# Two masked attention layers on one core: the first batch's load and scaling order, and the last batch's input steps

## The chip, the cores and the metric

The program runs on one core of one Trainium2 chip. The metric is the device time of one execution in microseconds (us); lower is better. The core has five engines that run side by side, each working through its own list of instructions strictly in the order in which the program wrote them: TensorE (PE in the profile; its weight loads are PEld), VectorE (DVE), ScalarE (ACT), GpSimd (POOL) and SyncE (SP), which here only issues DMAs. An instruction that waits for another engine or for a DMA holds up everything behind it on its own engine.

## The reference

Sixteen batches of 1024 rows by 256 features go through two layers. Each layer normalises its input, cuts it at zero, runs masked attention (4 heads of 64 in layer 0, 8 heads of 32 in layer 1) and adds the result to the input:

```python
h = jnp.maximum(_layernorm(x, axis=-1), 0.0)
x = x + gnn0(h, adj)
h = jnp.maximum(_layernorm(x, axis=-1), 0.0)
x = x + gnn1(h, adj)
# gnn: q, k, v = h @ Wq (+bq), h @ Wk (+bk), h @ Wv (+bv), split by heads
scores = jnp.where(adj > 0, q @ k.T / sqrt(D), -inf)
out = softmax(scores) @ v, heads joined, @ Wo.T + bo
```

Everything is 32-bit. `adj` is an integer matrix of 1024 by 1024 for each batch, the same for both layers.

## The kernel before

**Attention steps.** The main work is a list of steps (`layer_steps`): 16 for layer 0 of a batch, 32 for layer 1. A batch's rows are two halves of 512; a step takes one group of heads, one half of the queries, and two key tiles of 128 (layer 0) or one (layer 1, four heads at a time). `scores` (L501) multiplies keys by queries into two PSUM pairs called `ps`; the pool of such pairs has three buffers, shared by all large products. `exponentials` puts the mask on each pair on VectorE (L524, output `p`) and then takes the exponential on ScalarE (L530). `weigh` (L542, output `po`) multiplies the exponentials with the values, two steps later. The sums of the exponentials are made by GpSimd adding tiles in pairs (L659), by an adding DMA that GpSimd issues (`accumulate`, L643), and by a product with ones on TensorE (`count`, L387, output `pz`). They then travel: copied by ScalarE (`spread`, tile `s`), moved by DMA (`sums`), inverted on VectorE (`vn`), sent out and fetched back by DMA (`vd`, `inv`), and multiplied into the output on GpSimd (`normalize`, L447, tile `cat`). `end_half` (L483, `py`) multiplies `cat` with Wo.

**Order of the steps.** Layer 0 of batch 0, then in turn layer 0 of batch b+1 and layer 1 of batch b, and at last layer 1 of batch 15. Below, c is the first step of layer 1 of batch 14, and e = c + 32 the first of layer 1 of batch 15.

**Work laid between the steps.** `later(i, f, ...)` puts a piece of work at step i. `Stream.run` (L588) writes step by step: scores; the weighing of earlier steps; counts; the exponentials; then the pieces due at this step, first those that `rank` does not name and then those that it does (`turn` and the `LARGE` ones: `k`, `q`, `values`, `end_half`). Layer 0 takes two steps at a time, so pieces due at steps 0 and 1 are written together. On an even step of layer 1 that carries a `LARGE` piece the weighing is put off to the next step. There is no scheduler behind this: the order written is the order run.

**Inputs of a layer** (`Inputs`, one for each batch and layer, work by halves): `stats` (L198, L199 on VectorE for each of four row tiles, then four small operations on GpSimd, L209 to L212, that give `rstd` and `shift`); `norm` (ScalarE, L221) or `scale` (VectorE, L243) into `hn`; a transposition to `hT`, either on TensorE (`turn`, `turn_scaled`, output `ph`, copied out by ScalarE and VectorE at L260 and L261) or in blocks on VectorE with two DMA trips (`turn_blocks`, `put_blocks`, `place_blocks`); then `k`, `q` (L304, `pq`) and `values` (L345, `pv`), each copied out of PSUM. `add_bias` (L230, GpSimd) adds the output bias to the rows.

**Masks.** `Mask.load` fetches one eighth of `adj` with four DMAs; `put` (L167, ScalarE) packs it; `flip` (L173, VectorE) transposes blocks; `second` (L178, ScalarE) rewrites it for layer 1. The first step needs eighths 0 to 3.

**The head** (L738 to L789, before the steps): loads are issued on SP, save eighths 1 and 3 of the first mask, which ScalarE issues. `idle(n)` (L755) is n products of the identity with itself into a tile that nothing reads. Then half 0 of batch 0 gets its statistics, `norm` for three tiles and `scale` for the fourth, `turn_scaled`, `k`, `q`; half 1 gets statistics, `scale` and `turn_scaled`, and its `k`, `values` and `q` are laid at steps 0 and 2. `norms(inputs[0][1], 0, 1, ...)` (L851) lays the first statistics of batch 1 at step 1.

**The tail's inputs** (the `else` at L889): statistics, `norm`, bias, transposition, `k`, `q` and `values` of layer 1 of batch 15 are laid over the 32 steps of layer 1 of batch 14.

Of the kernel before, what the change touches and what calls it, by code (L numbers as in the profile page):

```python
# [24 lines left out]
LARGE = ("k", "q", "values", "end_half")  # L25
# [65 lines left out]
def fast_program(ctx, tc, a, w, loads, chk):  # L91
# [3 lines left out]
    nc = tc.nc  # L95
    x, adj, out = a["x"], a["adj"], a["out"]
    B, N, E = x.shape
    NT = N // P
# [35 lines left out]
    def open_x(b, half):  # L134
        t = xp.tile([P, 4, E], F32, tag=f"x{half}", name=f"x_{b}_{half}")
        for g, rows in enumerate(quarters(x, b, half)):
            nc.sync.dma_start(t[ts(g, 32)], rows)
        xs[b, half] = t


    class Mask:
# [3 lines left out]
        def load(self, u, at=None, queue=nc.sync):  # L145

            if at is None:
                at = adjp.tile([P, 4, 256], I32, tag="adj", name=f"adj_{self.b}_{u}")
            self.src[u] = at
            rows = adj[self.b].rearrange("(t h r g) (k c) -> h t k r g c", h=QH, r=32, g=4, k=4)  # L150
            for k in range(4):
                queue.dma_start(at[ts(k, 32)], rows[u // 4, u % 4, k])
# [415 lines left out]
    class Stream:  # L568
# [12 lines left out]
        def later(self, i, f, *args):  # L581
            self.due.setdefault(i, []).append((f, args))

        def rank(self, entry):

            return entry[0].__name__ in ("turn", *LARGE)

        def run(self):  # L588
            steps = self.steps
# [143 lines left out]
    def open_w(n):  # L733
        for _ in range(n):
            t, src = loads.pop(0)
            nc.sync.dma_start(t, src)
# [3 lines left out]
    mask, inp = masks[0], inputs[0][0]  # L740
# [8 lines left out]
    def rewrite(u):  # L749
        mask.put(u)  # L750
        mask.flip(u)
# [3 lines left out]
    def idle(n):  # L755
        for _ in range(n):
            nc.tensor.matmul(warm[:, 0, :P], w.ident, w.ident, start=True, stop=True)

    idle(22)
    open_w(2)  # L760
    for u in (1, 3):
        load(u, nc.scalar)
    open_x(0, 1)
    for u in (0, 2):
        load(u)
    open_w(1)
    for u in range(4, NT):
# [5 lines left out]
    inp.stats(0, (0, 1), True)  # L773
    inp.stats(0, (2, 3), True)
    inp.norm(0, (0, 1, 2), whole=True)
    inp.stats(1, (0, 1))
    inp.scale(0, (3,))
    inp.turn_scaled(0, lambda: idle(7))
    idle(3)
    inp.stats(1, (2, 3))  # L780
    rewrite(0)
    mask.put(1)
    inp.k(0)
    mask.flip(1)
    inp.scale(1, range(4))
    rewrite(2)
    rewrite(3)
    inp.q(0)
    inp.turn_scaled(1)  # L789

    def bias_of_v():

# [22 lines left out]
    later = stream.later  # L815

    def norms(inp, half, *at, whole=False, bias=None):

        for i, f in zip(at, (inp.stats, inp.stats, inp.norm, inp.norm)):
            rest = (whole,) if i in at[2:] else ()  # L820
            later(i, f, half, (0, 1) if i in (at[0], at[2]) else (2, 3), *rest)
        later(at[3] + 1 if bias is None else bias, inp.add_bias, half)

    def half_inputs(inp, half, *at):

        for i, f in zip(at, (inp.turn, inp.k, inp.q, inp.values)):
            later(i, f, half)

    def block_inputs(inp, half, turn, put, place, *at):

        later(turn, inp.turn_blocks, half)
        later(put, inp.put_blocks, half)
        later(place, inp.place_blocks, half)
        for i, f in zip(at, (inp.k, inp.q, inp.values)):
            later(i, f, half)


    for i, f, half in (0, inp.k, 1), (0, inp.values, 0), (0, inp.values, 1), (2, inp.q, 1):
        later(i, f, half)
    for half in range(QH):  # L840
        later(10 + 2 * half, inp.add_bias, half)
# [3 lines left out]
    for t in range(NT):  # L845
        i = 7 + 2 * t
# [8 lines left out]
    for b in range(B - 1):  # L855
        mine, a, c = inputs[1][b], first[b + 1], second[b]
        if b == 0:

            norms(mine, 0, a + 4, a + 6, a + 7, a + 8, whole=True)
            half_inputs(mine, 0, a + 10, a + 12, a + 13, a + 14)  # L860
            norms(mine, 1, a + 10, a + 11, a + 12, a + 13, whole=True)
            half_inputs(mine, 1, a + 15, c, c + 6, c + 2)
        else:
            norms(mine, 0, a - 20, a - 16, a - 15, a - 13, bias=a)
            block_inputs(mine, 0, a - 10, a - 8, a - 4, a, a + 2, a + 8)
            norms(mine, 1, a - 14, a - 10, a - 8, a - 6, bias=a + 6)
            block_inputs(mine, 1, a, a + 6, a + 7, c, c + (6 if b + 2 < B else 10), c + 2)
        for i, u in zip((0, 2, 4, 6, 7, 9, 11, 13), range(NT)):
            later(a + i, masks[b].second, u)
        if b + 2 < B:  # L870
            other, mask = inputs[0][b + 2], masks[b + 2]
            later(a + 6, open_x, b + 2, 0)
            later(c, open_x, b + 2, 1)
            if b == 0:
                norms(other, 0, a + 12, a + 14, c, c + 1, bias=c + 34)
                block_inputs(other, 0, c + 2, c + 3, c + 4, c + 8, c + 16, c + 18)
                norms(other, 1, c + 3, c + 4, c + 6, c + 7, bias=c + 36)
                block_inputs(other, 1, c + 8, c + 9, c + 12, c + 22, c + 26, c + 30)
            else:
                norms(other, 0, a + 10, a + 12, a + 13, a + 15, bias=c + 34)  # L880
                block_inputs(other, 0, c, c + 1, c + 2, c + 8, c + 16, c + 18)
                norms(other, 1, c + 2, c + 4, c + 5, c + 6, bias=c + 36)
                block_inputs(other, 1, c + 7, c + 8, c + 12, c + 22, c + 26, c + 30)
            at = 5, 8, 10, 12, 14, 45, 49, 51, 53
            for t in range(NT):
                later(a + at[t], mask.load, t)
                later(a + at[t + 1], mask.put, t)
                later(a + at[t + 1] + (1 if t == 4 else 2), mask.flip, t)
        else:  # L889
            last, e = inputs[1][b + 1], c + 32  # L890
            norms(last, 0, c + 5, c + 6, c + 8, c + 9)
            block_inputs(last, 0, c + 12, c + 13, c + 14, c + 18, c + 26, c + 20)
            norms(last, 1, c + 18, c + 20, c + 21, c + 22)
            block_inputs(last, 1, c + 24, c + 25, c + 26, e, e + 10, e + 2)
            for i, u in zip((4, 14, 24, 26, 36, 40, 42, 44), range(NT)):
                later(c + i, masks[b + 1].second, u)
    stream.run()

# [155 lines left out]
def kernel(  # L1054
# [28 lines left out]
    with ExitStack() as fast, tc.manual_schedule():  # L1083
        fast_program(fast, tc, a, w, loads, chk)
# [61 lines left out]
```

## Time and profile before

| what | value |
|---|---|
| median of three runs | 3099.81 us (3097.14 to 3100.33) |
| profiled execution, its own time | 3096.61 us |
| its span in the profile | 3094.8 us |
| VectorE, ScalarE, GpSimd busy | 2474.6, 2230.1, 2436.5 us |
| mean granted TensorE clock | 0.999 |
| median time from issue to landing, `adj` and `x` loads on SP | 3.0 and 3.1 us |
| one batch in the steady part (steps of batch 3 to 4, layer 0 to layer 0) | 189.6 us |

The span is the time from the first to the last recorded instruction; some 1.8 us of the execution lie outside it. In the profile's lists a row reads: start, duration (both us), engine, line, operation, output and inputs, shapes, number of instructions merged, and in brackets the engine's idle time before it with what ended it. A "q" behind an engine's name is its sequencer, which issues a DMA. Matmuls of 32-bit data appear as more than one record each. Matmul ends are modelled, so a stretch in which TensorE waits between two products of one group can still count as busy.

### The profile page before, as it was taken

The page shows a single profiled execution, that of the slowest core. Times are in us where ns is not written, and L with a number is a line of the kernel's source. Part 1 is how long each engine was busy: PE and PEld are TensorE (multiplying, and loading weights), DVE is VectorE, ACT ScalarE, POOL GpSimd, SP SyncE. Part 2 cuts the span into 40 slices and gives each one's busy share as a digit, 9 for nine tenths or more (in the row PEclk, how much of TensorE's full clock was granted, in tenths as well). Part 3 has the DMA queues.
Part 4 walks back from the last instruction along what each step waited for, and adds up shares of the span by engine and source line. Part 5 has one row for each costly group of instructions (what it writes and reads, how often), then busy time and mean ns, then how long its engine had stood idle before and what let it go on. Part 6 is the DMA issues. An engine that isn't in the chain of part 4 may idle for free.

```text
span 3094.8 us, 47328 instructions
## 1 busy us (share of the span) xinstructions
PE 3074.0 (99%) x17406; PEld 1221.3 (39%) x17406; DVE 2474.6 (80%) x2698; ACT 2230.1 (72%) x2436; POOL 2436.5 (79%) x1554
## 2 busy tenths in 40 slices
PE   9999999999999999999999999999999999999998
PEld 4443433434334343343434334343343433434333
DVE  6778788887888878788787888878788787887777
ACT  5677777777777777778677677776777777776676
POOL 3578878787887878878788787887878778787787
PEclk9999999999999999999999999999999999999999
DMA  5215545454463544635445353554535545453331
GB/s 129 66 58 118 127 106 129 121 112 119 107 137 110 119 118 103 143 108 117 120 103 134 107 127 110 113 127 110 127 110 111 132 105 125 120 112 84 79 77 33
DMA packets 259230, 341.37 MB, mean 110 GB/s; under 512 B 58288, under 2 KB 218288, under 8 KB 241968
## 3 DMA queue, kind: packets, MB, share of 16 engines
q0 software_dynamic: 19152, 139.47, 22.6%
q1 hardware_dynamic: 238368, 197.51, 22.2%
q8 instruction: 138, 2.26, 0.3%
q10 hardware_dynamic: 1472, 1.31, 0.2%
q14 instruction: 100, 0.82, 0.1%
HBM read 149.95 MB, written 47.96 MB: 64 GB/s over the span
## 4 chain that ended last, share of the span: by engine, by line
PE 95%; DVE 2%; POOL 1%; DMA 1%; issue 1%; ACT 0%; SPq 0%; DVEq 0%; ACTq 0%; POOLq 0%
PE ps L501 31%; PE po L542 29%; PE pq L304 15%; PE pv L345 8%; PE py L483 7%; PE pz L387 4%; DVE p L524 1%; POOL p L659 1%; DMA inv<-vd 0%; DMA x<-in_x_dram 0%; SPq L420 0%; ACT p L530 0%; DMA sums<-s 0%; POOL cat L447 0%; DMA adj<-in_adj_dram 0%
## 5 line engine op out<-in xcount | busy, mean ns | idle before, releaser
L524 DVE SCALAR_TENSOR_TENSOR p<-mask,ps 128x1024 f32<-128x1024 fp8e5 x1536 | 1791.9, 1214 | 366.2 <-PE ps L501 348.5
L530 ACT ACTIVATE p<-p 128x1024 f32<-128x1024 f32 x1536 | 1607.0, 1056 | 628.1 <-DVE p L524 572.1
L659 POOL TENSOR_TENSOR p<-p,p 128x1024 f32<-128x1024 f32 x510 | 1212.8, 2430 | 166.3 <-PE po L542 165.8
L501 PE MATMUL ps<-qT,kT 32*128 32x512 f32 (+1 forms) x6144 | 1073.3, 628 | 3.6 <-DVE p L524 3.0
L542 PE MATMUL po<-p,v 128*32 128x512 f32 (+1 forms) x6144 | 980.2, 600 | 0.7 <-ACT cat L399 0.4
L501 PEld LDWEIGHTS ps<-qT,kT 32*128 32x128 f32 (+1 forms) x6144 | 349.7, 184 | 587.9 <-issue 243.1
L542 PEld LDWEIGHTS po<-p,v 128*32 128x32 f32 (+1 forms) x6144 | 234.3, 118 | 680.3 <-issue 474.5
L555 POOL TENSOR_TENSOR p<-p 128x1024 f32<-128x1024 f32 x128 | 302.7, 2365 | 90.5 <-DVE p L554 85.1
L554 POOL TENSOR_TENSOR p<-p,p 128x1024 f32<-128x1024 f32 x64 | 150.8, 2356 | 169.6 <-DVE p L551 126.3
L345 PE MATMUL pv<-wv,hT 128*128 128x256 f32 x1024 | 237.8, 385 | 0.0
L304 PE MATMUL pq<-hT,wk 128*128 128x512 f32 x512 | 236.7, 605 | 0.7 <-DVE p L524 0.6
L304 PE MATMUL pq<-hT,wq 128*128 128x512 f32 x512 | 236.6, 605 | 0.1
L483 PE MATMUL py<-wo,cat 128*128 128x256 f32 x1008 | 234.4, 386 | 0.7 <-DVE p L524 0.6
L447 POOL TENSOR_TENSOR cat<-cat,inv 128x512 f32<-128x512 f32 x127 | 174.9, 1383 | 73.0 <-DMA inv<-vd 72.6
L345 PEld LDWEIGHTS pv<-wv,hT 128*128 128x128 f32 x1024 | 189.4, 190 | 72.1 <-DVE p L524 21.3
L483 PEld LDWEIGHTS py<-wo,cat 128*128 128x128 f32 x1008 | 186.3, 190 | 74.8 <-issue 25.1
L551 DVE TENSOR_TENSOR p<-p 128x1024 f32<-128x1024 f32 x128 | 181.7, 1419 | 0.0
L387 PE MATMUL pz<-p,ones 128*32 128x256 f32 (+1 forms) x1928 | 180.4, 444 | 0.5 <-DMA p<-p 0.5
L643 POOL DMA_DIRECT2D p<-p x133 | 122.6, 922 | 63.7 <-POOL p L659 30.3
L221 ACT ACTIVATE hn<-x,shift,rstd 128x256 f32<-128x256 f32 x251 | 135.6, 588 | 43.7 <-DMA turned<-hn 32.2
L399 ACT COPY cat<-po 128x512 f32<-128x512 f32 x128 | 73.4, 573 | 118.5 <-PE py L483 96.6
L488 DVE TENSOR_TENSOR x<-py,x 128x1024 f32<-128x1024 f32 x63 | 77.1, 1224 | 101.9 <-PE py L483 101.2
(62 smaller groups left out, 1773.1 us busy)
## 6 DMA issues: line engine op xcount, KB each, us to landing
p<-p POOLq DMA_DIRECT2D x133, 1024.0 KB, 7.8
adj<-in_adj_dram SPq DMA_DIRECT2D x504, 128.0 KB, 3.0
turned<-hn SPq DMA_DIRECT2D x58, 512.0 KB, 3.8
hT<-turned SPq DMA_DIRECT2D x232, 128.0 KB, 2.8
x<-in_x_dram SPq DMA_DIRECT2D x128, 128.0 KB, 3.1
inv<-vd SPq DMA_DIRECT2D x128, 128.0 KB, 3.0
inv<-vd SPq DMA_DIRECT2D x252, 64.0 KB, 3.3
out_dram<-x SPq DMA_DIRECT2D x124, 128.0 KB, 2.3
```

What stands on the lines that cost most here:

```text
L304: nc.tensor.matmul(pq[:, m, :], wt[self.layer][:, c, ts(m, P)], self.hT[half][:, c, :], start=(c == 0), stop=(c == 1),)
L345: nc.tensor.matmul(pv[:, i, :], self.hT[half][:, c, ts(i, P)], w.v[self.layer][:, c, :], start=(c == 0), stop=(c == 1),)
L387: nc.tensor.matmul(self.s[ts(r, 32), q], w.ones.to_broadcast([P, 32]), of[:, q], start=start and not part, stop=stop and part != 0,)
L447: nc.gpsimd.tensor_mul(o, o, inv)
L483: nc.tensor.matmul(py[:, i, :], self.half.cat[:, c, ts(i, P)], w.o[self.layer][:, c, :], start=(c == 0), stop=(c == 1),)
L501: nc.tensor.matmul(st.ps[i // 2][:, i % 2, :], gr.inp.kT[r * D : (r + 1) * D, gr.g, ts(kt, P)], gr.inp.qT[gr.qh][r * D : (r + 1) * D, gr.g ...
L524: nc.vector.scalar_tensor_tensor(out=half, in0=gr.mask.m[gr.qh][:, kt // 4, :, kt % 4].unsqueeze(1).to_broadcast([P, 2, 512]), scalar=-EDG ...
L530: nc.scalar.activation(half, half, AF.Exp, scale=gr.scale)
L542: nc.tensor.matmul(gr.o[r * D : (r + 1) * D, :], gr.inp.v[:, kt, h * D : (h + 1) * D], st.halves[i // 2][:, i % 2, :], start=(kt == 0), st ...
L551: nc.vector.tensor_add(a, a, b)
L555: nc.gpsimd.tensor_add(a, a, b)
L659: nc.gpsimd.tensor_add(half, half, of)
```

## The change

In the head, all loads of the first mask go to SP, eighths 0 and 1 ahead of the second half of `x`, eighths 2 and 3 behind it. The `scale` of the fourth tile comes before any statistics of half 1; those come as one call after the first `k`. The idle products inside the first transposition go from 7 to 3. `turn_scaled` of half 1 leaves the head: two of its tiles are scaled there and two at step 0, and the transposition stands at step 0 behind `values` of half 0 and ahead of `k` of half 1. The mask's `rewrite` calls (a `put` and a `flip` each) stand otherwise among the products. `rank` counts `turn_scaled` with the large pieces.

In the tail, `q` of half 1 of layer 1 of batch 14 goes from step c+10 to c+8. For layer 1 of batch 15 the statistics of a half, laid two tiles at a time at c+5, c+6 and c+18, c+20, become one call at c+8 and at c+20; `norm` goes to c+11, c+12 (half 0) and c+22 (half 1, all four tiles); the bias of half 0 from c+10 to c+13; transposition, DMA out and DMA back from c+12, c+13, c+14 to c+14, c+15, c+16, and from c+24, c+25, c+26 to c+26, c+27, c+28; `k`, `q`, `values` of half 0 from c+18, c+26, c+20 to c+20, c+22, c+26. Two `second` calls are moved.

```diff
         def rank(self, entry):
-            return entry[0].__name__ in ("turn", *LARGE)
+            return entry[0].__name__ in ("turn", "turn_scaled", *LARGE)
...
     idle(22)
     open_w(2)
-    for u in (1, 3):
-        load(u, nc.scalar)
+    for u in (0, 1):
+        load(u)
     open_x(0, 1)
-    for u in (0, 2):
+    for u in (2, 3):
         load(u)
     open_w(1)
     for u in range(4, NT):
...
     inp.norm(0, (0, 1, 2), whole=True)
-    inp.stats(1, (0, 1))
     inp.scale(0, (3,))
-    inp.turn_scaled(0, lambda: idle(7))
+    inp.turn_scaled(0, lambda: idle(3))
     idle(3)
-    inp.stats(1, (2, 3))
     rewrite(0)
-    mask.put(1)
+    rewrite(1)
     inp.k(0)
-    mask.flip(1)
-    inp.scale(1, range(4))
+    inp.stats(1)
     rewrite(2)
+    inp.q(0)
     rewrite(3)
-    inp.q(0)
-    inp.turn_scaled(1)
+    inp.scale(1, (0, 1))
...
-    for i, f, half in (0, inp.k, 1), (0, inp.values, 0), (0, inp.values, 1), (2, inp.q, 1):
+    later(0, inp.scale, 1, (2, 3))
+    for i, f, half in (
+        (0, inp.values, 0), (0, inp.turn_scaled, 1), (0, inp.k, 1), (0, inp.values, 1),
+        (2, inp.q, 1),
+    ):
         later(i, f, half)
...
-            block_inputs(mine, 1, a, a + 6, a + 7, c, c + (6 if b + 2 < B else 10), c + 2)
+            block_inputs(mine, 1, a, a + 6, a + 7, c, c + (6 if b + 2 < B else 8), c + 2)
...
             last, e = inputs[1][b + 1], c + 32
-            norms(last, 0, c + 5, c + 6, c + 8, c + 9)
-            block_inputs(last, 0, c + 12, c + 13, c + 14, c + 18, c + 26, c + 20)
-            norms(last, 1, c + 18, c + 20, c + 21, c + 22)
-            block_inputs(last, 1, c + 24, c + 25, c + 26, e, e + 10, e + 2)
-            for i, u in zip((4, 14, 24, 26, 36, 40, 42, 44), range(NT)):
+            later(c + 8, last.stats, 0)
+            later(c + 11, last.norm, 0, (0, 1))
+            later(c + 12, last.norm, 0, (2, 3))
+            later(c + 13, last.add_bias, 0)
+            block_inputs(last, 0, c + 14, c + 15, c + 16, c + 20, c + 22, c + 26)
+            later(c + 20, last.stats, 1)
+            later(c + 22, last.norm, 1)
+            later(c + 23, last.add_bias, 1)
+            block_inputs(last, 1, c + 26, c + 27, c + 28, e, e + 10, e + 2)
+            for i, u in zip((4, 8, 14, 26, 36, 40, 42, 44), range(NT)):
                 later(c + i, masks[b + 1].second, u)
```

## The prediction

> **What bounds the kernel now.** First the page's busy times and its chain of waits, by engine:
>
> ```profile
> PE 3074.0 (99%) x17406; PEld 1221.3 (39%) x17406; DVE 2474.6 (80%) x2698; ACT 2230.1 (72%) x2436; POOL 2436.5 (79%) x1554
> PE 95%; DVE 2%; POOL 1%; DMA 1%; issue 1%; ACT 0%; SPq 0%; DVEq 0%; ACTq 0%; POOLq 0%
> ```
>
> TensorE is busy 99% and is 95% of the chain: 20.8 us are left to gain in all. The table by stretch says where (columns: stretch, length, busy time and count of PE, PEld, DVE, ACT, POOL, granted clock, DMA share, GB/s):
>
> ```profile
> 0.00:24.20 24.20, 19.92 (x98) 14.85 (x98) 9.34 (x29) 9.10 (x12) 4.81 (x24) 0.93 0.91 218
> 7.96:11.38 3.42, 0.98 (x7) 0.57 (x6) 1.02 (x4) 1.51 (x3) 2.31 (x8) 1.00 1.13 234
> 11.38:14.79 3.41, 3.41 (x17) 3.06 (x15) 1.24 (x5) 0.08 (x1) 0.00 (x0) 0.50 1.12 231
> 2421.80:2611.60 189.80, 189.77 (x1075) 75.03 (x1074) 153.75 (x168) 139.27 (x152) 153.43 (x98) 1.00 0.48 117
> 2875.00:2900.00 25.00, 23.70 (x146) 8.74 (x143) 20.34 (x25) 18.47 (x22) 19.37 (x14) 1.00 0.29 65
> ```
>
> A steady batch has nothing to give: 189.77 of 189.80 us. The head and layer 1 of batch 14 (2858 to 2971) have, and only these are changed. The middle only shifts by what the head gains or loses. Now the head's timeline:
>
> ```profile
> 9.78 5.21 SPq L152 DMA_DIRECT2D adj<-in_adj_dram  x8
> 15.66 10.74 SPq L152 DMA_DIRECT2D adj<-in_adj_dram  x16
> 26.45 2.01 SPq L137 DMA_DIRECT2D x<-in_x_dram  x4
> 13.45 0.43 DVE L198 BATCH_NORM_STATS2 st<-x 128x6 f32<-128x256 f32 x1 [4.36 <-DMA x<-in_x_dram]
> 31.63 0.43 DVE L198 BATCH_NORM_STATS2 st<-x 128x6 f32<-128x256 f32 x1 [1.50 <-DMA x<-in_x_dram]
> 16.25 3.70 PE L304 MATMUL pq<-hT,wk 128*128 128x512 f32 x8
> 24.19 3.74 PE L501 MATMUL ps<-qT,kT 64*128 64x512 f32 x16
> 27.93 3.70 PE L304 MATMUL pq<-hT,wk 128*128 128x512 f32 x8
> 31.46 7.07 PE L345 MATMUL pv<-wv,hT 128*128 128x256 f32 x32
> 38.46 3.70 PE L501 MATMUL ps<-qT,kT 64*128 64x512 f32 x16
> ```
>
> VectorE waits twice for `x`: at 13.45 for half 1 of batch 0, with the fourth tile's `scale` (14.69) behind it, so the first `k` starts only at 16.25; and at 31.63 for batch 1, which costs nothing, since TensorE has `k` and `values` until 38.46.
>
> **The head, part by part.** *Before the first `k`.* The first four `x` loads take 2.5 us to land where they have little company, and the last was late: statistics start at 6.40. Without ScalarE's loads I put that at 4.9 (last issue 2.1 plus 2.6), 1.4 earlier. The later `shift` moves from 10.44 to 9.0, `norm` and `scale` end at 9.6 (0.59 each), 6 idle records take 0.75 (as the 6 at 15.4), the last transposes 0.63, the copy 0.60: first `k` near 11.3, 5 us earlier.
>
> *What eats it.* `k` and `q` (7.1) end at 18.6, scores can start at 19.3. The masks are next: eighth 3 is still the last of the same 3.5 MB and lands near 19.3 (SP issues it until 15.6, plus 3.7); `put` 1.13, `flip` 0.43, two `scale` 0.75 bring the first masking to 21.8, against 25.53. Four maskings (4.6) end at 26.4. `values` of half 0 waits for a pair that the second masking frees (24.1) and ends at 27.8; the transposition, now here, ends at 28.7 (0.87); ScalarE's copy (0.60, behind 1.01 of copying values) at 29.5.
>
> *The new wait.* `k` of half 1 needs both copies of `hT`; VectorE's (L261) is written behind the pieces that `rank` does not name at steps 0 and 1, and one of these is the statistics of batch 1, the row at 31.63. So VectorE stands at a DMA, behind it `hT`, behind that `k` on TensorE, and behind that everything. With a the arrival of that `x`: two statistics 1.33 (31.63 to 32.96), copy 0.73, then three quarters of `k` 2.78 and `values` 3.46, and 0.05 of hand-over: next scores at a + 8.35, against 38.46. The gain of 5 us becomes idle time of TensorE between 30.4 and a + 2.1.
>
> *How late is a?* SP issues the mask at 0.65 each (5.21/8) and takes eight more of them: 5.2. But it stood waiting before: the four `x` loads took 3.81 and another 1.17 passed before 9.78, together with a 0.8 gap ahead of `wq`. Counted anew: `wq` done at 3.5, 5.2 for eight, 2.0 for four `x` (as at 26.45): 10.7 instead of 9.78, and from there the same list. Latency should be a little less on an emptier queue. I take 0.4 later, a = 32.0, head +1.9 (40.35 against 38.46). Bounds: all 5.2 late, a = 36.8, +6.7; or, with the fifty loads of 128 KB up to it (6.55 MB) at the 246 GB/s that the stretch from 1.5 to 8.2 shows with both queues, a = 28.1, where `k` waits for `hT`'s own copies alone (30.4) and the head gains 1.9.
>
> The Trainium skill ("Trainium Kernel Development and Optimization", Key Constraints) holds that issuing DMAs from several engines saves nothing but sequencer time. By it the move would cost at most SP's 5.2, and nothing where the 16 engines are full; the rows show both in part (DMA share 1.13 at 8 to 11 us, 0.64 at 24 to 28), and the counted 0.9, less some latency, stands.
>
> *Clock.* That gap is 3.7 us. In the rows above, 0.98 us of work in 3.42 was followed by 3.41 us at half clock. In the new gap two such lengths hold some 1.1 to 1.2 us of work each (up to 28.7 with 0.9 of `k`; after 34.15). Bounds 0 and 2.3 (both next lengths at half clock while work waits: 0.6 and 1.7). I take 1.7, as the nearest row is the halved one. The skill ("TensorE: Matmul & The Clock Gate", The two states you'll see) wants a whole idle window of about 3.4 us, free-running, before the clock drops; a 3.7 us gap would seldom hold one, and the sum would be 1.7 lower. The row, halved with 29% busy, goes against that reading. Head: +3.6.
>
> **Layer 1 of batch 14.** Its waits, in the timeline:
>
> ```profile
> 2887.40 1.13 PE L501 MATMUL ps<-qT,kT 32*128 32x512 f32 x4 [0.55 <-DVE p L524]
> 2890.88 1.13 PE L501 MATMUL ps<-qT,kT 32*128 32x512 f32 x4 [0.29 <-DVE p L524]
> 2896.51 2.52 POOL L447 TENSOR_TENSOR cat<-cat,inv 128x512 f32<-128x512 f32 x2 [0.41 <-DMA inv<-vd]
> 2903.98 0.91 POOL L643 DMA_DIRECT2D p<-p  x1 [0.30 <-POOL p L659]
> 2906.97 9.60 POOL L659 TENSOR_TENSOR p<-p,p 128x1024 f32<-128x1024 f32 x4
> 2911.99 0.64 PE L387 MATMUL pz<-p,ones 128*32 128x256 f32 x8
> 2913.24 1.13 PE L483 MATMUL py<-wo,cat 128*128 128x256 f32 x4 [0.60 <-DVE p L524]
> ```
>
> Scores stall where VectorE has statistics between maskings; later GpSimd is the pace. Steps 7 and 8 lose about 2.7 us now (ps to po 2.74 and 2.48, against 1.07 unhindered). New: step 6 stays, since `vn` waits for `sums` until 2886.0 with or without statistics ahead; step 7's maskings come 1.2 earlier; step 8 has `q` (3.70) over four statistics (2.7) and the `qT` copy (1.41). Step 11 starts 0.6 earlier than 2901.23. But GpSimd now does `ve` behind all four statistics, which end near 2895.9: 1.6 for L209 to L212, 2.5 for `cat`, 4.7 for the next addition: 2904.75 against 2903.70. The adding DMA is issued 1.05 later and landed 7.3 after its issue; the count that needs it moves from 2911.99 to 2912.45, `py` to 2913.05: 0.2 gained of 1.2. The bias (2.67) behind the next four additions puts the following ones at 2919.4, against 2919.18. In steps 15 to 20, now with no large product, both maskings and additions need 2.35 a step against 2.07 on TensorE; `k` at step 20 covers that. Transposed rows reach `hT` near 2965, `k` wants them after 2970. Sum: -0.5. Bounds: all the idle of 2875 to 2975 gone (3.4: 1.30, 1.32 and 0.82 in its stretches), or both halves with four statistics ahead of GpSimd's queue (1.05 and 1.35 late): +2.4. I stay by the worked row, since GpSimd holds either way.
>
> **Sum.** +3.6 and -0.5: +3.1 on 3096.61, 3099.7; the profiled execution lies 3.2 below the median, so the same shift gives 3102.9.
>
> **The rivals.** *The head's gain survives*: `x` of batch 1 lands by 28.3. For it: 246 GB/s early on; against: 0.65 an issue on one queue, and SP's list before it is the same. -1.9, with the tail -0.5 to -3.4: 3094.5 to 3097.4.
>
> *Slower beyond telling*: SP carries the eight loads in full, a = 36.8. For it: 5.21 us for eight; against: SP's own waits in 3.0 to 9.8. Head +6.7, half clock +1.7, tail -0.5: 3107.7; it decides from a = 35.0 (+4.9 head, with the rest +6.1).
>
> *The tail is not evened*: GpSimd late in both halves, +3.6 +2.4: 3105.8. For it: `ve` ahead of `cat` and the additions; against: GpSimd's idle 2.25 and 1.11 us at 2932 and 2940, which takes the second half's.
>
> **How the numbers follow.** A measurement of this kernel can tell some 0.2%, 6.2 us, from no change. Forecast 0.62 (0.60 within, 0.02 slower), gain survives 0.18 (0.06 faster, where both lower bounds, -5.3 together, meet the 3 us by which runs differ; 0.12 within), late loads 0.13 (0.10 slower, 0.03 within), uneven tail 0.07 (0.02 slower, 0.05 within). Faster 0.06, within 0.80, slower 0.14. Range: low 3095.5, inside the first rival, high 3107, short of the late loads.
>
> **What would show it.** First `k` near 11 to 12; a wait of VectorE for `x` of 4 us or more ahead of L198 near 32, then L261, then `k` of half 1 ending near 37; scores of step 2 near 40.4, perhaps at clock 0.5; step 14's `py` at most 1.2 us earlier relative to the layer's start. If those statistics start by 28, or TensorE has no gap ahead of that `k`, the forecast's mechanism is wrong.

## The result, and the profile after

The changed kernel takes **3105.36 us** (median of 20 runs, 3100.99 to 3107.00); the kernel before, on the same chip, 3097.72 us (20 runs, 3095.62 to 3100.33). The ratio is **1.0022**, with a 95% interval of 1.0015 to 1.0029: slower by 7.6 us, where 3.1 had been forecast. The time lies inside the predicted range (3095.5 to 3107). The loss is over the 6.2 us that the prediction called the least that can be told from no change, but its interval, 4.6 to 9.0 us, holds that bound. The profiled execution took 3104.45 us, its span is 3102.6 us, against 3096.61 and 3094.8 before.

The busy times by engine and the chain of waits by engine, of the kernel after:

```profile
PE 3075.2 (99%) x17398; PEld 1220.8 (39%) x17398; DVE 2467.5 (80%) x2698; ACT 2231.3 (72%) x2436; POOL 2437.9 (79%) x1554
PE 91%; DVE 2%; DMA 2%; POOL 1%; ACT 1%; issue 1%; SPq 1%; DVEq 0%; ACTq 0%; POOLq 0%
```

TensorE is still busy 99% of the span, but its share of the chain went from 95% to 91%: DMAs, ScalarE and SP's queue have each about a point more of it. To see where the time went, the span is cut at four places that both kernels have: the first scores of step 2, of layer 0 of batch 1, of layer 1 of batch 14, and of layer 1 of batch 15. The table by stretch, first of the kernel before, then after (stretch, length, busy time and count of PE, PEld, DVE, ACT, POOL, granted clock, DMA share, GB/s):

```profile
111.99:2858.01 2746.02, 2743.80 (x15385) 1085.59 (x15384) 2229.47 (x2423) 2003.99 (x2192) 2199.14 (x1391) 1.00 0.47 115
2858.01:2970.70 112.69, 109.88 (x707) 39.93 (x705) 87.69 (x92) 80.61 (x88) 95.24 (x57) 1.00 0.38 89
2970.70:3094.80 124.10, 113.01 (x870) 43.15 (x866) 87.24 (x83) 79.94 (x84) 93.53 (x58) 0.98 0.16 39
```

```profile
117.62:2866.44 2748.82, 2744.41 (x15385) 1085.59 (x15384) 2221.71 (x2423) 2004.75 (x2192) 2200.24 (x1391) 1.00 0.47 115
2866.44:2976.59 110.15, 107.82 (x706) 39.32 (x704) 88.02 (x92) 80.90 (x88) 95.18 (x57) 1.00 0.40 90
2976.59:3102.60 126.01, 114.06 (x870) 43.55 (x866) 87.25 (x83) 79.94 (x84) 93.55 (x58) 0.96 0.16 40
```

With the head (scores of step 2 at 38.46 before, 43.94 after) and the short piece up to batch 1 (73.53 and 73.68 us), the 7.8 us between the spans divide as follows:

| part | predicted | seen in the two profiles |
|---|---|---|
| head, up to the scores of step 2 | +3.6 | +5.5 |
| from there to layer 0 of batch 1 | 0 | +0.15 |
| middle, whose code is the same in both | 0 | +2.8 |
| layer 1 of batch 14 | -0.5 | -2.5 |
| layer 1 of batch 15 to the end | 0 | +1.9 |

The head's timeline of the kernel after:

```profile
11.32 3.70 PE L304 MATMUL pq<-hT,wk 128*128 128x512 f32 x8
27.46 2.01 SPq L137 DMA_DIRECT2D x<-in_x_dram  x4
27.29 1.04 PE L259 MATMUL ph<-ident,hn 128*128 128x128 f32 x8
29.05 1.12 PE L304 MATMUL pq<-hT,wk 128*128 128x512 f32 x2 [0.73 <-ACT hT L260]
32.86 0.43 DVE L198 BATCH_NORM_STATS2 st<-x 128x6 f32<-128x256 f32 x1 [6.28 <-DMA x<-in_x_dram]
34.10 0.66 DVE L261 TENSOR_SCALAR hT<-ph 128x512 f32<-128x512 f32 x1
34.81 5.49 PE L304 MATMUL pq<-hT,wk 128*128 128x512 f32 x6 [4.64 <-DVE hT L261]
40.09 3.92 PE L345 MATMUL pv<-wv,hT 128*128 128x256 f32 x16
43.94 3.27 PE L501 MATMUL ps<-qT,kT 64*128 64x512 f32 x14
```

The first `k` starts at 11.32, five microseconds earlier than before. `k` of half 1 starts at 29.05, and after a quarter of it TensorE stands for 4.64 us. The bracket names VectorE's copy of `hT` (L261), which itself took 0.66 us; it stood behind the statistics of batch 1 (L198), and these stood 6.28 us for `x`, which SP issued only at 27.46. The rest of `k` then took 5.49 us for six records, where eight take 3.70: it ran at half clock.

### The profile page after: what moved, and what is told of

Its sections match the earlier page's. It is cut to its first block, busy times and chain, and to the rows that moved or that the text cites. A ratio compares the mean times of both kernels' runs of the same rounds, so it can differ in the third digit from the quotient of the medians.

```text
span 3102.6 us, 47318 instructions
## 1 busy us (share of the span) xinstructions
PE 3075.2 (99%) x17398; PEld 1220.8 (39%) x17398; DVE 2467.5 (80%) x2698; ACT 2231.3 (72%) x2436; POOL 2437.9 (79%) x1554
## 3 DMA queue, kind: packets, MB, share of 16 engines
q8 instruction: 139, 2.28, 0.3%
## 4 chain that ended last, share of the span: by engine, by line
PE 91%; DVE 2%; DMA 2%; POOL 1%; ACT 1%; issue 1%; SPq 1%; DVEq 0%; ACTq 0%; POOLq 0%
PE ps L501 30%; PE po L542 28%; PE pq L304 14%; PE py L483 7%; PE pv L345 7%; PE pz L387 4%; DVE p L524 1%; DMA inv<-vd 1%; DMA sums<-s 1%; POOL p L659 1%; DMA turned<-hn 0%; ACT p L530 0%; SPq L420 0%; DMA p<-p 0%; SPq L439 0%
```

## The experiments

All times are medians beside runs of the kernel before on the same chip. The idle products that some add or take away write a tile that nothing reads.

**1. Statistics of batch 1 one step later.** In the kernel after:

```diff
-    norms(inputs[0][1], 0, 1, 3, 5, 6, whole=True)
+    norms(inputs[0][1], 0, 2, 3, 5, 6, whole=True)
```

> The changed kernel with one number altered: the first statistics of batch 1 laid at step 2 in place of step 1, so that VectorE copies hT of half 1 before it waits for x of batch 1. Wait theory (the loss is VectorE standing at that DMA, then half clock): k of half 1 has no wait over 1 us, no half clock between 30 and 45 us, the scores of step 2 start near 36.3 us against 43.9 in the changed kernel and 38.5 before, and the time falls by about 7.6 us to 3097 to 3099. Load theory (all loads on one queue are late and that is the loss): scores of step 2 still past 42 us and the time stays at 3104 to 3106. Tail theory (the late statistics of batch 15 are the loss): the head improves as above but the time stays over 3102.

Measured: 3096.37 us (11 runs) against 3098.41, ratio 0.9995 (0.9986 to 1.0004). Its head:

```profile
29.39 0.69 DVE L261 TENSOR_SCALAR hT<-ph 128x512 f32<-128x512 f32 x1 [2.45 <-ACT hT L260]
29.41 3.70 PE L304 MATMUL pq<-hT,wk 128*128 128x512 f32 x8 [0.73 <-ACT hT L260]
32.95 3.62 PE L345 MATMUL pv<-wv,hT 128*128 128x256 f32 x16
36.49 3.70 PE L501 MATMUL ps<-qT,kT 64*128 64x512 f32 x16
```

VectorE now copies `hT` at 29.39, as soon as the transposed tiles are there, `k` runs through, and step 2's scores start at 36.49 instead of 43.94. One piece of work laid one step later took away the whole loss: the time is the same as before within its interval. So the wait for `x` of batch 1 costs the head 7.45 us, clock included, and without it the head's new order gains 2 us on the profile of before (38.46).

**2 and 3. Each half of the change alone.** Experiment 2 has the head of before and the tail of after (with `q` at c+8); experiment 3 the head of after and the tail of before.

```diff
 # 3: the tail as before
-            later(c + 8, last.stats, 0)
...
+            norms(last, 0, c + 5, c + 6, c + 8, c + 9)
+            block_inputs(last, 0, c + 12, c + 13, c + 14, c + 18, c + 26, c + 20)
```

> The kernel before with the change's tail alone (head as before). By the traces layer 1 of batch 14 takes 2.5 us less (110.2 against 112.7), so wait theory: 3094 to 3096, 2 to 3 us under before. Tail theory: over before, 3099 or more. If the 1.9 us lost after layer 1 of batch 14 in the changed kernel's trace belongs to the tail, the sum is -0.6 and the time the same as before within a microsecond.

> The kernel before with the change's head alone (tail as before). Wait theory: scores of step 2 near 43.9 us and the time 3103 to 3106 by the head's 5.5 us alone, up to 3108 if the tail's gain of 2.5 us is missing from it. Tail theory: time near before, under 3100.

Measured: tail alone 3095.65 against 3098.41, 0.9991 (0.9982 to 1.0000); head alone 3106.07 against 3098.41, 1.0025 (1.0016 to 1.0034). The tail gains about 2.8 us, though its interval just reaches no change, and the head loses about 7.7, so the loss comes with the head. The two add up to 4.9 us, not to the 7.6 of the whole change. The intervals, some 3 us either way, leave room for that, but the profiles show a part that comes only with both: from layer 1 of batch 15 to the end takes 123.78 us with the tail alone, 124.48 with the head alone and 126.01 and 125.64 in the two profiles of the kernel after. Layer 1 of batch 14 takes 110.90 us with the tail alone and 113.06 with the head alone.

**4. Work in the gap.** In the kernel after, 20 idle products stand between the transposition of half 1 and `k`, in the time in which TensorE waits:

```diff
-        (0, inp.values, 0), (0, inp.turn_scaled, 1), (0, inp.k, 1), (0, inp.values, 1),
-        (2, inp.q, 1),
+        (0, inp.values, 0), (0, inp.turn_scaled, 1), (0, fill, 20), (0, inp.k, 1),
+        (0, inp.values, 1), (2, inp.q, 1),
```

> The changed kernel with 20 idle products (5.5 us) on TensorE between the transposition of half 1 and its k: the wait for hT stays, but TensorE has work in it. If the half clock of 6.8 us after the gap is due to the gap, it does not come, and scores of step 2 start near 41.2 us (32.9 + 8.35) in place of 43.9: 2.5 to 3 us less than the changed kernel, 3102 to 3103. If the clock falls for another reason, no gain: 3105.

Measured: 3099.25 against 3098.41, 1.0000 (0.9991 to 1.0009). This was expected at 3102 to 3103. First the kernel after, by stretches at which the clock can change (in all fourteen profiles a granted clock holds for a multiple of 3.413 us, save the last, which the end cuts off; columns as above):

```profile
27.04:30.45 3.41, 2.41 (x12) 1.24 (x11) 0.00 (x0) 1.51 (x2) 0.00 (x0) 1.00 0.73 229
30.45:33.86 3.41, 0.00 (x0) 0.00 (x0) 0.93 (x3) 0.00 (x0) 0.00 (x0) 1.00 0.70 197
33.86:37.27 3.41, 2.46 (x3) 1.17 (x4) 0.86 (x3) 0.00 (x0) 0.00 (x0) 0.50 0.95 213
37.27:40.69 3.42, 3.42 (x6) 1.52 (x5) 0.00 (x0) 0.35 (x1) 0.00 (x0) 0.50 1.04 309
```

Then the timeline of the experiment, and its stretch from `k` to the scores:

```profile
28.52 4.63 PE L762 MATMUL fill<-ident 128*128 128x128 f32 x40
32.71 0.43 DVE L198 BATCH_NORM_STATS2 st<-x 128x6 f32<-128x256 f32 x1 [5.76 <-DMA x<-in_x_dram]
34.66 2.84 PE L304 MATMUL pq<-hT,wk 128*128 128x512 f32 x6 [0.65 <-DVE hT L261]
37.34 3.62 PE L345 MATMUL pv<-wv,hT 128*128 128x256 f32 x16
```

```profile
34.66:40.89 6.23, 6.23 (x23) 4.10 (x23) 0.00 (x0) 1.01 (x1) 0.00 (x0) 1.00 1.07 287
```

VectorE's statistics start at 32.71, as in the kernel after (32.86), so the wait is the same; but the six records of `k` take 2.84 us instead of 5.49, and the scores start at 40.89. That is 32.71 + 8.18, against the prediction's a + 8.35 with full clock. The empty stretch of 30.45 to 33.86 thus cost the kernel after two lengths of 3.41 us at half clock, and 43.94 - (32.86 + 8.35) = 2.7 us (2.9 by the 8.18). The time fell by more than that: the 20 products also move what stands behind them, and experiments 9 to 12 come back to this.

**5 and 6. The loads alone.** Experiment 5 is the kernel before with only the head's loads in the new order; experiment 6 the kernel after with the loads in the old one.

```diff
 # 5 (6 is the reverse, in the kernel after)
-    for u in (1, 3):
-        load(u, nc.scalar)
+    for u in (0, 1):
+        load(u)
     open_x(0, 1)
-    for u in (0, 2):
+    for u in (2, 3):
         load(u)
```

> The kernel before with only the order of the loads changed: all on SP, eighths 0 and 1 ahead of the second half of x. Wait theory: the loads alone cost nothing that is seen, since x of batch 1 has slack there: its statistics start near 32.9 us in place of 31.6, TensorE does not wait for them, scores of step 2 at 38 to 40 us, time within 1.5 us of before. Load theory (one queue is itself the loss): scores of step 2 past 42 us and the time 4 us or more over before.

> The changed kernel with the loads as they were, on two queues. Wait theory: the wait for x of batch 1 stays, since VectorE's order is the change's, but x comes some 1.2 us sooner: scores of step 2 at 40 us without the half clock, 42.7 to 43.4 with it; time 3102 to 3105, at most 2.5 us under the changed kernel. Load theory: the loss is gone, 3098 or less.

Measured: experiment 5 3100.20 against 3098.21, 1.0005 (0.9996 to 1.0015); experiment 6 3100.05 against 3098.21, 1.0006 (0.9996 to 1.0015). The second was expected at 3102 to 3105: a miss. The first was expected within 1.5 us of before and lies 2.0 over it, with no change inside its interval; its scores of step 2, expected at 38 to 40, start at 41.05, behind two lengths at half clock in its head (13.94 to 20.77) where the kernel before has one. The timelines of 5 and of 6:

```profile
32.70 0.43 DVE L198 BATCH_NORM_STATS2 st<-x 128x6 f32<-128x256 f32 x1
34.05 7.07 PE L345 MATMUL pv<-wv,hT 128*128 128x256 f32 x32
41.05 3.70 PE L501 MATMUL ps<-qT,kT 64*128 64x512 f32 x16
```

```profile
31.45 0.43 DVE L198 BATCH_NORM_STATS2 st<-x 128x6 f32<-128x256 f32 x1 [1.68 <-DMA x<-in_x_dram]
32.24 4.01 PE L304 MATMUL pq<-hT,wk 128*128 128x512 f32 x8 [0.73 <-ACT hT L260]
36.08 3.62 PE L345 MATMUL pv<-wv,hT 128*128 128x256 f32 x16
39.63 2.85 PE L501 MATMUL ps<-qT,kT 64*128 64x512 f32 x12
```

In 5 the statistics start as late as in the kernel after, and TensorE does not stop: nothing that it needs stands behind them. The new loads by themselves cost nothing that could be told from no change. In 6 the wait is there, but the first `k` comes 2.4 us later than in the kernel after (13.73 against 11.32) and `x` 1.4 us earlier (31.45), so the gap closes to fragments, no stretch of 3.41 us has under 2.3 us of work there, and the clock stays. The scores start at 39.63, again a + 8.18. Both kernels also show what the early `k` is made of: with the new loads alone it starts at 17.11, with the new order of work alone at 13.73, with both at 11.32.

**7 and 8. The kernel before and the kernel after once more.**

> The kernel before once more, for a second trace of its middle (from layer 0 of batch 1 to layer 1 of batch 14, code that the change does not touch), which took 2746.0 us in the first trace and 2748.8 in the changed kernel's. If the 2.8 us are run to run spread, this one lies anywhere from 2744 to 2749; if the middle follows the head, 2744.5 to 2746.5.

> The changed kernel once more, for a second trace of its middle, 2748.8 us in the first. If that is spread, anywhere from 2744 to 2749; if the middle follows the head, 2747.5 to 2749.5.

Measured, one execution each: 3099.77 and 3105.0 us. The middle took 2746.20 and 2747.66 us, against 2746.03 and 2748.82 in the first profiles. Two of a kind do not settle it, but every profile with the kernel after's head so far (experiments 1, 3 and 6) had a middle of 2747.87 to 2748.09, every one with the kernel before's (2 and 5) 2744.65 to 2745.29, and experiment 4, with 20 products added to the head of after, 2746.14.

**9 and 10. The number of idle products.** The kernels differ there in one more thing: 7 idle products against 3 inside the first transposition. Experiment 9 is experiment 1 with `idle(7)`, experiment 10 the kernel before with `idle(3)`:

```diff
 # 9, in experiment 1 (10 is the reverse, in the kernel before)
-    inp.turn_scaled(0, lambda: idle(3))
+    inp.turn_scaled(0, lambda: idle(7))
```

> The changed kernel with the first statistics of batch 1 at step 2, as tried before, and with 7 idle products inside the first transposition in place of 3, as in the kernel before. In nine traces the middle (layer 0 of batch 1 to layer 1 of batch 14) took 2744.7 to 2746.2 us where TensorE's program has 7 idle products in its head and 2747.7 to 2748.8 where it has 3, and 2746.1 with 3 and 20 more. Position theory: the middle follows the number of TensorE instructions ahead of it, so 2744.5 to 2746.5 here, and the time falls to 3093 to 3095, under the kernel before by 3 to 5 us. Timetable theory: the middle follows how far ahead or behind the other engines stand after the head, so 2747.5 to 2749 and a time of 3096 to 3097. Scores of step 2 at 36 to 37 us in both.

> The kernel before with 3 idle products in place of 7 inside the first transposition, nothing else. Position theory: its middle takes 2747.5 to 2749 us in place of 2744.7 to 2746.2 and the time rises by 2 to 3 us to 3100 to 3101.5. Timetable theory: middle and time as before (2744.5 to 2746.5; 3097 to 3099).

Measured: experiment 9 **3094.30** (11 runs) against 3098.28, 0.9988 (0.9979 to 0.9997), faster than both kernels; middle 2745.61. Experiment 10 3102.54 against 3098.28, 1.0014 (1.0004 to 1.0023); middle 2747.55. The middles are as the theory of position had them. Experiment 10 lost 4.3 us, more than the 3 expected and more than its middle explains; in its profile layer 1 of batch 14 also has two lengths at half clock and takes 114.94 us, against 112.69 and 113.60 in the profiles of before.

**11 and 12. The same number elsewhere.** To part position from what the products do to the transposition, the warm-up ahead of everything gets 4 more in the kernel after (11), and 4 fewer in the kernel before (12); the transposition is left alone.

```diff
 # 11, in the kernel after (12: idle(18), in the kernel before)
-    idle(22)
+    idle(26)
```

> The kernel after, with 26 idle products in place of 22 ahead of everything, so that as many products as in the kernel before stand ahead of the first batch; the first transposition keeps its 3. Theory that the length of the unchanged middle (layer 0 of batch 1 to layer 1 of batch 14) follows the number of TensorE instructions ahead of it, wherever they stand: middle 2744.5 to 2746.5 us, as in the five profiles with 7 idle products; step 2's scores still near 44, as in the kernel after, since x of batch 1 decides them; the whole some 2.4 below the kernel after, near 3103. Rival, that the products inside the transposition matter by what they do to the head's times or clock: middle 2747.5 to 2749, the whole near 3105.4.

> The kernel before, with 18 idle products in place of 22 ahead of everything; the transposition keeps its 7. Theory that the number of instructions ahead decides: middle 2747.5 to 2749, the whole 2 to 2.5 above the kernel before, near 3100.5, with the head as before (step 2's scores 38.5 to 40.4). Rival, that it is the place of the products: middle 2744.5 to 2746.5, the whole near 3098.

Measured: experiment 11 3100.60 against 3098.64, 1.0008 (0.9999 to 1.0018), middle 2745.44, and the scores of step 2 at 43.98 as expected; experiment 12 3101.92 against 3098.64, 1.0011 (1.0002 to 1.0021), middle 2747.46. For the middle the number decides, not the place: four short products in the first 10 us, eight TensorE records, change a middle that starts a hundred microseconds later by 1.3 to 3.4 us. The whole times missed, 3100.60 for 3103 and 3101.92 for 3100.5, so the four products move more than the middle. By the four pairs (1 and 9, before and 10, after and 11, before and 12) they are worth 2 to 6 us in the whole, each known to 3 or 4 us; where the rest lies was not followed up. Over all fourteen profiles:

| idle products ahead | middle, us |
|---|---|
| as before (2, 5, 9, 11 and the kernel before twice) | 2744.65, 2745.29, 2745.61, 2745.44, 2746.03, 2746.20 |
| four fewer (1, 3, 6, 10, 12 and the kernel after twice) | 2747.91, 2747.87, 2748.09, 2747.55, 2747.46, 2748.82, 2747.66 |
| sixteen more than before (4) | 2746.14 |

What they shift is seen in layer 0 of batch 5. The timelines of SP, VectorE and TensorE, first of the kernel after, then of experiment 11:

```profile
922.99 3.81 SPq L152 DMA_DIRECT2D adj<-in_adj_dram  x4
926.89 2.44 SPq L420 DMA_DIRECT2D sums<-s  x4
930.98 0.25 DVE L428 RECIPROCAL vn<-sums 128x16 f32<-128x16 f32 x1 [2.42 <-DMA sums<-s]
932.37 1.13 PE L501 MATMUL ps<-qT,kT 64*128 64x512 f32 x4 [1.09 <-DVE p L524]
```

```profile
922.74 2.49 SPq L152 DMA_DIRECT2D adj<-in_adj_dram  x4
925.33 2.44 SPq L420 DMA_DIRECT2D sums<-s  x4
928.94 0.25 DVE L428 RECIPROCAL vn<-sums 128x16 f32<-128x16 f32 x1 [0.63 <-DMA sums<-s]
928.19 3.70 PE L501 MATMUL ps<-qT,kT 64*128 64x512 f32 x16
```

In the kernel after SP needed 3.81 us to issue four mask loads, 2.49 in the other; the sums of the exponentials left 1.3 us later than SP's start explains, VectorE's reciprocal waited 2.42 instead of 0.63, the masking behind it was late, and TensorE stood 1.09 us. The table of DMA queues for 922 to 928 us of the kernel after names one packet that is no data; the last two rows are from the table of the whole execution:

```profile
q1 hardware_dynamic: 460, 0.42, 24.5%
q8 instruction: 1, 0.02, 1.4%
q8 instruction: 139, 2.28, 0.3%
q14 instruction: 101, 0.83, 0.1%
```

The first queue of that name, q8, moves 139 packets of 16 KB in the execution, one every 22 us, 2.28 MB in all; the packets meant below are these. With 34,796 records of TensorE (products and weight loads) that is a packet for each 250, so it looks to be TensorE's own program; the trace doesn't name its owner. In the same 6 us experiment 11 has none. In the kernel after, experiment 3 and experiment 1, and in the second profile of after, the packet falls 8.3 to 8.6 us ahead of that step of batch 5 and 3.4 to 3.8 us ahead of the like step of batch 9, and TensorE stands there 0.51 to 1.09 us; with the four products back it falls elsewhere in batch 5, some 2 us earlier in batch 9, and neither wait is there; of the six profiles with the number as before one alone has a wait at either place, 0.24 us in batch 9 (the second of the kernel before). In the other three profiles with four fewer (experiments 6, 10 and 12) both waits are there, of 0.15 to 0.20 and 0.41 to 1.08 us. At the like step of batch 2 it is the other way round: in the six profiles with the number as before a packet falls 4.0 to 4.5 us ahead of the scores and TensorE stands 0.18 to 0.46 us, in the others it does not.

Counted over the middles of all fourteen profiles, a mask load whose issue overlaps such a packet took over 0.9 us to issue in 89 of 206 cases (mean 0.92), one that does not in 503 of 6178 (mean 0.65).

TensorE's idle time in the middle, as the trace has it, is 4.41 us in the kernel after and 2.35 in experiment 11; that is 2.1 of the 3.4 us between their middles. The kernel after has the most of all; the means are 3.4 us over the seven profiles with four fewer and 2.3 over the six with the number as before. Another 1.1 us lies at the end of layer 1 of batch 12: in all seven profiles with four fewer a packet falls late in the time in which the last sums are on their way (at 2590.55 in the kernel after, which issues them at 2584.65), these need 8.6 to 9.0 us from issue to landing instead of 7.4 to 7.9 in the seven others, the reciprocal waits for them (2.76 us in the kernel after), and eight records of scores behind it are spread over 2.25 us instead of 1.14, which the trace counts as busy. The means of the seven less those of the six, step by step, put the 2.4 us in few places: the last two steps of layer 1 of batch 12 (+1.2), the steps named of batches 5 and 9 (+0.8 and +0.7), one in layer 1 of batch 7 (+0.3), and the one of batch 2 (-0.6). In both kernels some groups of TensorE products also run 0.3 to 0.4 us longer than their like, at steps 28 and 29 of layer 1, in batches 2 and 9 in the one and in batches 4 and 11 in the other; these cancel, and what makes them was not found. That the packets cause the waits is argued from where they fall; it was not shown by a kernel that changes them alone.

## Why the prediction was right, and where it was not

**First `k`: right.** Statistics at 4.9, first `k` near 11.3 were predicted; 5.05 and 11.32 were measured. The pieces listed there add up to 11.6, so agreement this close is luck. Experiments 5 and 6 share the gain out between the loads and the order.

**The new wait: right in kind and nearly in size.** VectorE stands for `x` of batch 1, `hT` behind it, `k` behind that, and the scores start at a + 8.35; with a full clock they started at a + 8.18 twice (experiments 4 and 6). The arrival a was put at 32.0 and came at 32.86; the other profiles with this head have 32.71 to 33.82. But the bound was not new: kernels with the old loads have 31.45 to 33.76, the kernel before 31.63 once and 32.72 once. What the new loads add, put at 0.4, is smaller than what arrivals differ by from run to run. The rival of SP's eight loads in full (a = 36.8) and that of the surviving gain (a below 28.3) both fell.

**"I take 1.7": the half clock was mis-sized.** One length of 3.41 us at half clock was taken, as in the row of before, with 2.3 for two lengths as the bound. It was two lengths, and 2.7 us, beyond that bound (two lengths in each of the four profiles with this gap, at 1.9 to 2.9 us against a + 8.18). The step that failed is that in the new gap "two such lengths hold some 1.1 to 1.2 us of work each": `x` came 0.86 us later and the first quarter of `k` earlier than thought, so the gap was 4.64 us and not 3.7, and one whole length was empty. Then half clock did not end after one length, as in the row of before, where TensorE worked all through it: the first length held 2.46 us of work, and a second followed. The Trainium skill ("TensorE: Matmul & The Clock Gate", The two states you'll see) was weighed in the prediction for its rule of one whole idle window; this gap holds such a window and was halved, as the rule has it, and experiment 6, without one, was not. But in experiments 3 and 11, with the same gap, the length ahead of half clock held 0.69 and 0.62 us of work, and the halving at the end of the kernel after, shown below, came behind 1.24 us: these go against it.

**"The middle only shifts by what the head gains or loses": wrong.** It took 2.8 us more in the two profiles compared, some 2.4 by the means of the table, and experiments 11 and 12 show that four idle products fewer do this. They were counted in the prediction as head work alone, and the middle was put at nothing without a look at what their number might do.

**Layer 1 of batch 14, -0.5: right in sign, mis-sized.** It gained 2.5 us. Predicted was that GpSimd holds: behind all four statistics it would issue the adding DMA 1.05 us later, and `py` of step 14 would come only 0.2 earlier in all. The timelines of GpSimd and TensorE of the kernel after:

```profile
2902.95 0.20 POOL L209 TENSOR_TENSOR ve<-mv,numbers 128x4 f32<-128x4 f32 x1 [0.86 <-DVE mv L199]
2912.01 0.90 POOL L643 DMA_DIRECT2D p<-p  x1 [0.30 <-PE ps L501]
2919.09 0.64 PE L387 MATMUL pz<-p,ones 128*32 128x256 f32 x8 [1.33 <-DMA p<-p]
2919.66 3.72 PE L483 MATMUL py<-wo,cat 128*128 128x256 f32 x16
```

From the start of the layer the statistics are done at 2902.95 - 2866.44 = 36.5 us, where 37.9 had been predicted. So the adding DMA is issued at 45.6 us and not near 47.0, 0.4 earlier than before instead of 1.05 later, and `py` of step 14 comes at 53.2 against 55.2: 2.0 us earlier, where at most 1.2 was allowed for. That GpSimd's adding DMA still ends the wait was right; VectorE's lead over it was underrated. Part of the gain has another source, which the first profile of before does not show: with the old tail the five other profiles each have one or two lengths at half clock inside this layer (3.4 us each, and 113.06 to 114.94 us for the layer), with the new tail one of eight has. No run took these halvings away by themselves.

**The end, +1.9: not foreseen.** The last part of the kernel after, by stretches, and the last output products, first of the kernel after, then of before:

```profile
3088.79:3092.20 3.41, 1.24 (x5) 0.82 (x6) 3.15 (x4) 0.00 (x0) 0.74 (x2) 1.00 0.03 2
3092.20:3095.61 3.41, 1.94 (x6) 1.04 (x6) 1.48 (x3) 0.00 (x0) 0.58 (x2) 0.50 0.00 0
```

```profile
3092.06 1.97 PE L458 MATMUL py<-wo,cat 128*128 128x256 f32 x4 [0.93 <-DVE cat L468]
3085.97 1.13 PE L458 MATMUL py<-wo,cat 128*128 128x256 f32 x4 [0.94 <-DVE cat L468]
```

The clock fell at 3092.20, just as the last output products (L458) started: they took 1.97 us instead of 1.13. Before, it fell at 3090.20, when they were done. That is 0.84 of the 1.9; another 0.87 lies behind the last stores' issue, in a piece that varies from 6.94 to 7.88 us over the profiles. The whole stretch is longer only with both halves of the change and the new loads: 125.17 to 126.01 us in these six profiles, 123.78 to 124.48 in the eight others. No run changed where the clock falls there, so why it comes with both stays open.

**The sum.** Against the prediction's 3.1 stand 7.6 us. The head's clock (1.0 more) and arrival (0.9 more), the middle (2.8) and the end (1.9) went against it, the tail (2.0 more gained) for it. The sum was also made on one profile of the kernel before whose head was early: its scores of step 2 came at 38.46, in the second profile at 40.41, and in the tail alone, with the same head, at 40.31. By these two the head of the kernel after lost some 3.6, not 5.5, and each term above holds to a microsecond or two and no better.

So the main mechanism was right, while the number was held by a wide range: the loss is two and a half times the forecast, two terms put at nothing (middle and end) cost 4.7 us, the tail's larger gain took 2.0 off again, and that the sum stayed under 3107 is partly luck. A loss that can be told from no change had been given 0.14, one within it 0.80.

## What to carry to other kernels

When an order is written out by hand, look at what is laid ahead of each copy that feeds the bounding engine: a piece for the next batch that waits for a load holds up the copy behind it, and one step later it need not (some 8 us here). Such a wait has a second price if it leaves a length of the clock's rhythm empty or nearly so, and idle products in the gap pay that off, though not the wait itself. And where effects are a thousandth of the time, change the number of instructions ahead by a few, in both kernels, before you give the difference to the edit: here four idle products were worth some 2 us in code that nobody had touched, and 2 to 6 us in the whole.

## What had not been expected of the hardware

- **Instruction packets share the DMAs' time.** Every 22 us a packet of 16 KB comes on a queue called "instruction" (q8). The Trainium skill ("Runtime: NRT & Kernel Launch", Instruction fetch mechanics) says that programs are streamed in blocks of 16 KiB, 256 instructions each, over a DMA queue, and that crossing a block is mostly hidden: the size and the 250 records for each packet agree. Where a packet falls near the sums it is not hidden here: TensorE stands 0.51 to 1.09 us in the four profiles named. SP's mask loads whose issue overlaps one took over 0.9 us to issue in 43% of the cases, others in 8%. The link from there to the middle's length rests on the steps named above and on moving the packets with four products; no kernel was run that changes the packets and nothing else.
- **Half clock does not ask for an empty stretch.** One of 0.98 us of work in 3.42 (before, at 7.96) and one of 1.24 in 3.41 (after, at 3088.79) were followed by half clock; so was one of 2.64, in the second profile of the kernel before:

```profile
2910.71:2914.12 3.41, 2.64 (x16) 0.67 (x14) 2.36 (x3) 1.52 (x2) 3.41 (x3) 1.00 0.62 201
```

  while one of 1.91 us, at 3083.37 of the first, was not. And at half clock 2.46 us of work in 3.41 did not bring the clock back, 3.42 did (the kernel after at 33.86 and 37.27). Over the fourteen profiles every length with at most 1.53 us of recorded TensorE work was followed by half clock, of those with 1.67 to 2.65 us some were, and none with more; at half clock no length with at most 2.64 us brought the clock back, and those with 2.74 us and more did. The busy time in the profile does not decide it alone; matmul ends are modelled there.
- **The kernel before's own head differs by 2 us** from run to run (scores of step 2 at 38.46 and 40.41), with the loads' arrival.
